# First quarters of A11 and A21 loaded apart, and the first k step's matmuls in another order

## The chip, the cores and the metric

The kernel runs on one core of a Trainium2 chip. The metric is the device time of one execution in microseconds. Three timed runs of the kernel before gave 414.72, 414.88 and 414.88 us, a median of 414.88.

The engines go by short names: TensorE is PE (its weight loads are PEld), VectorE is DVE, ScalarE is ACT, GpSimd is POOL, and SyncE, which here only issues DMAs, is SP. ACT and POOL issue DMAs too.

## The reference

The input `x` is 64 blocks of 64 x 1024 float32. Every block has a condition that picks one of 16 matrices of 64 x 64. The result is `x` plus a small feed-forward layer of the conditioned blocks:

```
W = weights[condition]                       # 64 blocks of 64 x 64
v = einsum('bct,bcd->bdt', x, W)             # conditioned input, flattened to 4096 x 1024
top1 = argmax(v @ gate_w.T + expert_bias)    # one of 4 experts for a row
z = einsum('nh,erh->ner', v, lora_A)         # 4 experts, rank 8
delta = einsum('ner,ehr->neh', z, lora_B)    # only the chosen expert's counts
out = x + v @ W_up.T + delta
```

All of it is float32.

## The kernel before

Two blocks of 64 rows make one tile of 128 rows, so there are 32 tiles (`NP`), handled as 16 pairs (`NG`). The condition is applied after the large product: for every tile the kernel first makes `x` times the joined matrix of gate, LoRA A and `W_up` (1024 x 1060, called B), and then multiplies the result by the tile's condition matrix.

For a pair of tiles the product is cut in two by rows (tile a, tile b), in two along the sum (512 each), and in two by columns (530 each, `NB`). That gives the blocks A11, A12 (tile a, first and second half of the sum), A21, A22 (tile b) and B11, B12, B21, B22. The first two pairs take the eight block products (`eight`, line 505); the others take seven with sums of blocks (`seven`, line 622). A block product runs over four k steps of 128 (`KH`), in `product` (line 214).

Float32 is done as three products: every operand is split into a high part (a rounded copy, `h...`, `ah`) and a low part (the rest, `l...`, `al`). ACT makes the high parts by a copy, DVE the low parts by a subtraction (`split_a`, `split_b`). `part_of_product` (line 198) issues the terms: term 0 is A high by B high, term 1 is A high by B low, term 2 is A low by B high. The 530 columns are done in two pieces of 264 and 266 (`BANKS`)[...]. So one k step of one block product is six matmuls, and the first k step of the first pair, which does A11 by B11 and A21 by B11 together, is twelve.

How a line is named: all engines are wrapped in `InOrder` (line 35), which keeps each engine's instructions in program order, so nearly every instruction of the trace is put down to line 43. Tile names tell them apart: `xx` holds the raw quarters of A11 and A21 (and later A12 and A22), `wraw` a raw k step of B, `hB` and `lB` the parts of B11, `ah` and `al` those of A, `c` the accumulators.

The start of the program is written out by hand. `keep_warm(WARM)` (lines 386 to 390) issues 30 matmuls of zeros on TensorE before any data is there. `load_halves` (line 393) loads, for one half of the sum and some k steps (`STEPS`, line 403), the quarters of A11 and A21 in one DMA; ACT issues the first and the second k step (lines 404 and 405), SP issues steps three and four later. SP loads B11's first k step in two pieces (lines 417 to 419), then B11's second k step, the rest of A11 and A21, the other k steps of B11, the second halves of A, and B21.

Then come the casts of the first k step, lines 436 to 450: ACT copies the first piece of B11, DVE makes A11's high part (by a maximum with itself, so that it need not wait for ACT), ACT copies the second piece of B11, DVE makes A11's low part and both low pieces of B11, ACT makes A21's high part and DVE its low part. The second k step's A follows.

The first block product is started in `run` (line 491). In `product`, with two block products at once, a k step goes: for A11 terms 0 and 2 in both pieces, then term 1 in both; then the same for A21. After the first k step the hooks of place (0, 0) in `eight` run: one more warming matmul, the split of B11's second k step, and `make_idx`, one small matmul on `condf` (the conditions, loaded by POOL into `cond_sb` at line 414 and cast by POOL), from which the row indices of the condition matrices are made.

Of the kernel before, what the change touches and what calls it, by code (L numbers as in the profile page):

```python
# [8 lines left out]
F32 = mybir.dt.float32  # L9
# [6 lines left out]
P = 128  # L16
KC = 8
KH = KC // 2
# [8 lines left out]

COLS = ((0, 356), (356, 352), (708, 352))
LAST = ((0, 356), (356, NB - 356), (NB, 258), (NB + 258, NB - 258))
WARM = 30  # L30
GATE = (("lg", E), ("mx", 1), ("sc", E), ("m2", 1), ("zm", ER))
HALVES = (slice(0, 64), slice(64, 128))

# [13 lines left out]
def kernel(  # L47
# [28 lines left out]
    tensor, vector, scalar, pool, sync = (  # L76
        InOrder(tc, e) for e in (nc.tensor, nc.vector, nc.scalar, nc.gpsimd, nc.sync)
    )
# [6 lines left out]
    yp = ctx.enter_context(tc.tile_pool(name="y", bufs=3))  # L85
# [5 lines left out]
    wh = {b: cpool.tile([P, KH, NB], F32R, name=f"h{b}") for b in BLOCKS}  # L91
    wl = {b: cpool.tile([P, KH, NB], F32R, name=f"l{b}") for b in BLOCKS}
# [3 lines left out]
    raw, As, us, ys, wsel, zs, os_, ts = ({} for _ in range(8))  # L96

    def temp(name):
        return tp.tile([P, NB], F32, name=name, tag="t")
# [23 lines left out]
    def source(g, name):  # L123
        return {
            "A11": (2 * g, 0),
            "A12": (2 * g, 1),
            "A21": (2 * g + 1, 0),
            "A22": (2 * g + 1, 1),
        }.get(name, (g, name))

    def split_a(g, name, k=slice(0, KH)):
        if (g, name) not in As:
            As[g, name] = [ap.tile([P, KH, P], F32R, name=m, tag=m) for m in ("ah", "al")]
        h, lo = As[g, name]
        src = raw[source(g, name)]
        scalar.copy(h[:, k], src[:, k])
        vector.tensor_sub(lo[:, k], src[:, k], h[:, k].bitcast(F32))


    def part(q, k):  # L140
        i, j = int(q[1]) - 1, int(q[2]) - 1
        return w[j][KH * i + k]

    def load_b(q, k):
        t = raw[q, k] = temp("wraw")
        sync.dma_start(t, part(q, k))
# [51 lines left out]
    def part_of_product(g, a, b, first, k, o, n, terms=(0, 1, 2)):  # L198
        h, lo = As[g, a]
        of = (h, wh[b]), (h, wl[b]), (lo, wh[b])  # L200
        for m in terms:
            tensor.matmul(
                o,
                of[m][0][:, k],
                of[m][1][:, k, n],
                start=first and k == 0 and m == 0,
                stop=k == KH - 1 and m == 2,
                skip_group_check=True,
            )

    BANKS = slice(0, CUT), slice(CUT, NB)
    LAST_BANKS = [slice(c0 - NB, c0 - NB + n) for c0, n in LAST[2:]]

    def product(g, which, hooks):

        turns = ((0, 1, 2),) if len(which) == 1 else ((0, 2), (1,))
        for k in range(KH):
            for c, a, b, first in which:
                for terms in turns:
                    for n in BANKS:  # L220
                        part_of_product(g, a, b, first, k, body(c)[:, n], n, terms)
            for kk, fn, *args in hooks:
                if kk == k:
                    fn(*args)

    def product_by_bank(g, places, a, b, hooks):

        for m, (o, n) in enumerate(zip(places, LAST_BANKS)):
            for k in range(KH):
                part_of_product(g, a, b, True, k, o[:, : n.stop - n.start], n)  # L230
                for kk, fn, *args in hooks:
                    if kk == KH * m + k:
                        fn(*args)

    def body(c):
        return c[:, LEFT : LEFT + NB]
# [149 lines left out]
    def keep_warm(n):  # L386
        for _ in range(n):
            tensor.matmul(wps[:, :P], warm, warm, start=True, stop=True)

    keep_warm(WARM)  # L390


    def load_halves(queue, hf, k):
        if k.start == 0:
            t = yp.tile([P, 2, KH, P], F32, name="xx", tag="y")
            for i in range(2):
                raw[i, hf] = t[:, i]
            raw["x", hf] = t
        queue.dma_start(
            raw["x", hf][:, :, k], xt[0:2, hf].rearrange("i p k q -> p i k q")[:, :, k]  # L400
        )

    STEPS = slice(0, 1), slice(1, 2), slice(2, KH)
    for k in STEPS[:2]:
        load_halves(scalar, 0, k)

    one = cpool.tile([P, 1], F32, name="one")
    vector.memset(one, 0.0)
# [2 lines left out]
    which = cpool.tile([2, P], I32, name="which")  # L411
# [7 lines left out]
    t = raw["B11", 0] = temp("wraw")  # L419
    pieces = slice(0, CUT), slice(CUT, NB)  # L420
    for n in pieces:
        sync.dma_start(t[:, n], part("B11", 0)[:, n])
    load_b("B11", 1)
    load_halves(sync, 0, STEPS[2])
    for k in range(2, KH):
        load_b("B11", k)
    load_halves(sync, 1, slice(0, KH))
    for k in range(KH):
        load_b("B21", k)
    def low(name, k):  # L430
        h, lo = As[0, name]
        vector.tensor_sub(lo[:, k], raw[source(0, name)][:, k], h[:, k].bitcast(F32))
# [3 lines left out]
    for name in ("A11", "A21"):  # L436
        As[0, name] = [ap.tile([P, KH, P], F32R, name=m, tag=m) for m in ("ah", "al")]
    t = raw["B11", 0]
    scalar.copy(wh["B11"][:, 0, p], t[:, p])
    u = raw[0, 0][:, k]  # L440
    vector.tensor_tensor(As[0, "A11"][0][:, k], u, u, ALU.max)
    scalar.copy(wh["B11"][:, 0, q], t[:, q])
    low("A11", k)
    for n in pieces:
        vector.tensor_sub(wl["B11"][:, 0, n], t[:, n], wh["B11"][:, 0, n].bitcast(F32))
    scalar.copy(As[0, "A21"][0][:, k], raw[1, 0][:, k])
    low("A21", k)
    for name in ("A11", "A21"):
        split_a(0, name, STEPS[1])

# [40 lines left out]
    def run(g, order, hooks, c):  # L491
        for s, step in enumerate(order):
            step = step if isinstance(step, list) else [step]
            for n, _, _, first in step:
                if first:
                    c[n] = chain()
            for kk, fn, *args in hooks[s]:
                if kk < 0:
                    fn(*args)
            product(g, [(c[n], l, r, first) for n, l, r, first in step], hooks[s])  # L500

    c = {}
# [328 lines left out]
```

## Time and profile before

| what | value |
|---|---|
| median of the timed runs | 414.88 us |
| profiled execution | 415.4 us |
| its span | 413.6 us |
| TensorE matmuls, busy | 408.5 us, 99% of the span |
| VectorE, ScalarE, GpSimd busy | 285.6, 185.0, 75.0 us |
| first matmul of zeros | 0.99 us |
| first matmul on data | 4.20 us |
| small matmul on `condf` | 7.26 us |
| first matmul of the second k step | 7.37 us |

The profile is of one execution, and its times count from the start of the span. A page lists the busy time of each engine, the span in slices, the chain of work that ended last, and the costliest groups of instructions. A timeline row gives the start, the duration, the engine, the line, the operation, what is written from what, the shape and the count; in brackets stands how long the engine was idle before it, and what ended the idle time. A name with a q behind the engine (SPq, ACTq) is a DMA being issued. The ends of matmuls are modelled, so durations of neighbouring matmuls overlap; the distance from start to start is what one costs.

### The profile page before, as it was taken

Reading aid. Unit: us, or ns where it says so; the run is one execution under the profiler, and the core shown is the slowest. Engines: PE = TensorE matmul, PEld = TensorE weight load, DVE = VectorE, ACT = ScalarE, POOL = GpSimd, SP = SyncE. Lnnn points to the kernel's source line nnn. Section 1 sums busy time; section 2 is a strip of 40 time slices with the busy share of each in tenths; the row PEclk is TensorE's granted clock in tenths of the full one; section 3 lists DMA queues with packets and bytes.
Section 4 is the critical chain, followed back from the end, with each engine's and each line's share of the span. In section 5 each row is a group of like instructions: output and inputs, shape, how many; then the busy total and the mean of one; then the engine's idle time right before and its main releaser. Section 6 shows DMA issues by size and latency. Waiting matters only on the chain.

```text
span 413.6 us, 8160 instructions
## 1 busy us (share of the span) xinstructions
PE 408.5 (99%) x3191; PEld 407.7 (99%) x3191; DVE 285.6 (69%) x648; ACT 185.0 (45%) x419; POOL 75.0 (18%) x92
## 2 busy tenths in 40 slices
PE   8999999999999999999999999999999999999996
PEld 8999999999999999999999999999999999999995
DVE  5987776876767666676676767666676676766766
ACT  5846734453534445333343534445333344533531
POOL 4304502020020202102020020202102020020000
PEclk9999999999999999999999999999999999999999
DMA  8889964553556435465453555434465443564345
GB/s 276 301 305 224 241 167 98 137 123 99 172 133 177 92 93 143 124 178 135 103 127 98 164 135 159 128 81 138 122 179 135 104 126 94 169 165 124 52 101 178
DMA packets 25830, 60.99 MB, mean 147 GB/s; under 512 B 3328, under 2 KB 5344, under 8 KB 25792
## 3 DMA queue, kind: packets, MB, share of 16 engines
q1 hardware_dynamic: 18112, 40.48, 27.2%
q0 software_dynamic: 6704, 19.21, 27.1%
q10 hardware_dynamic: 976, 0.79, 0.6%
q8 instruction: 25, 0.41, 0.4%
q14 instruction: 13, 0.11, 0.1%
HBM read 43.68 MB, written 16.78 MB: 146 GB/s over the span
## 4 chain that ended last, share of the span: by engine, by line
PE 97%; DMA 1%; issue 0%; POOL 0%; DVE 0%; POOLq 0%
PE c L43 81%; PE o L43 16%; DMA cond_sb<-in_cond_dram 1%; DVE y L43 0%; POOL which L43 0%; POOL condf L43 0%; POOLq L43 0%; POOLq L818 0%
## 5 line engine op out<-in xcount | busy, mean ns | idle before, releaser
L43 PE MATMUL c<-hT,ah 128*128 128x264 f32 x480 | 139.7, 291 | 0.0
L43 PE MATMUL c<-lT,ah 128*128 128x264 f32 x480 | 137.3, 286 | 0.0
L43 PE MATMUL c<-hT,al 128*128 128x264 f32 x480 | 137.1, 286 | 0.0
L43 PE MATMUL c<-hB,ah 128*128 128x264 f32 (+1 forms) x424 | 121.8, 289 | 0.0
L43 PE MATMUL c<-hB,al 128*128 128x264 f32 (+1 forms) x424 | 121.0, 287 | 0.0
L43 PE MATMUL c<-lB,ah 128*128 128x264 f32 (+1 forms) x424 | 119.0, 287 | 0.0
L43 PEld LDWEIGHTS c<-lT,ah 128*128 128x128 f32 x480 | 91.0, 190 | 0.0
L43 PEld LDWEIGHTS c<-hT,ah 128*128 128x128 f32 x480 | 90.9, 189 | 0.0
L43 PEld LDWEIGHTS c<-hT,al 128*128 128x128 f32 x480 | 90.6, 189 | 0.0
L43 POOL DMA_DIRECT2D y<-in_x_dram x31 | 29.3, 945 | 290.3 <-ACT y L43 285.3
L43 PEld LDWEIGHTS c<-hB,ah 128*128 128x128 f32 x424 | 80.7, 190 | 0.3 <-ACT hB L43 0.2
L43 PEld LDWEIGHTS c<-hB,al 128*128 128x128 f32 x424 | 80.7, 190 | 0.0
L43 PEld LDWEIGHTS c<-lB,ah 128*128 128x128 f32 x424 | 79.5, 190 | 0.2 <-issue 0.2
L43 ACT COPY y<-o 128x352 f32<-128x352 f32 (+1 forms) x91 | 40.1, 443 | 58.4 <-PE o L43 55.0
L43 ACT CAST uh<-usum 128x530 fp32r<-128x530 f32 (+4 forms) x44 | 27.1, 616 | 68.4 <-DVE usum L43 68.4
L43 DVE TENSOR_TENSOR al<-S,ah 128x512 fp32r<-128x512 f32 x56 | 38.5, 688 | 24.2 <-ACT ah L43 24.2
L43 DVE TENSOR_TENSOR al<-xh,ah 128x512 fp32r<-128x512 f32 x46 | 31.7, 689 | 30.0 <-ACT ah L43 30.0
L43 PE MATMUL o<-uh,bd 128*128 128x356 f32 (+2 forms) x186 | 44.7, 322 | 0.0
L43 DVE TENSOR_TENSOR ul<-usum,uh 128x530 fp32r<-128x530 f32 (+4 forms) x44 | 30.0, 682 | 18.6 <-ACT uh L43 18.6
L43 ACT CAST zt<-o 96x128 fp32r<-96x128 f32 x31 | 8.1, 262 | 76.0 <-PE o L43 76.0
L43 POOL DMA_INDIRECT wsel<-in_cw_dram,idx x32 | 34.9, 1089 | 10.6 <-issue 5.2
L43 ACT CAST ah<-S 128x512 fp32r<-128x512 f32 x56 | 34.9, 623 | 1.8 <-DVE S L43 1.4
(88 smaller groups left out, 471.3 us busy)
## 6 DMA issues: line engine op xcount, KB each, us to landing
xh<-in_xt_dram SPq DMA_DIRECT2D x60, 256.0 KB
y<-in_x_dram POOLq DMA_DIRECT2D x30, 512.0 KB, 5.6
out_dram<-y SPq DMA_DIRECT2D x30, 512.0 KB
wraw<-in_w_dram SPq DMA_DIRECT2D x23, 265.0 KB
T<-in_w_dram POOLq DMA_DIRECT2D x8, 265.0 KB, 7.3
xx<-in_xt_dram SPq DMA_DIRECT2D x1, 512.0 KB
wsel<-in_cw_dram,idx POOLq DMA_INDIRECT x32, 5.0
y<-in_x_dram SPq DMA_DIRECT2D x1, 512.0 KB
```

The costliest lines, as they stand in the source:

```text
L43: return lambda *a, **k: self.tc.keep_in_program_order(fn(*a, **k))
```

## The change

The first quarters of A11 and A21 are loaded by two DMAs instead of one, both still issued by ACT. The second quarters, still one DMA for both, are issued by SP, between the second piece of B11's first k step and B11's second k step. `WARM` goes from 30 to 26. The casts of the first k step are put in another order on ACT and DVE: A21's high part comes before the second piece of B11 on ACT, A21's low part before the second low piece of B11 on DVE. The twelve matmuls of the first k step are issued by a new function, `first_step`, in a written order; each entry is the block product (0 is A11, 1 is A21), the piece and the terms. Their number and operands are the same.

```diff
-WARM = 30
+WARM = 26
...
         for k in range(KH):
-            for c, a, b, first in which:
-                for terms in turns:
-                    for n in BANKS:
-                        part_of_product(g, a, b, first, k, body(c)[:, n], n, terms)
+            if g == 0 and k == 0 and which[0][2] == "B11":
+                first_step(which)
+            else:
+                for c, a, b, first in which:
+                    for terms in turns:
+                        for n in BANKS:
+                            part_of_product(g, a, b, first, k, body(c)[:, n], n, terms)
...
+    def first_step(which):
+
+        p, q = BANKS
+        for m, n, terms in (
+            (0, p, (0, 2)),
+            (1, p, (0,)),
+            (0, p, (1,)),
+            (1, p, (1,)),
+            (0, q, (0, 2)),
+            (1, q, (0,)),
+            (1, p, (2,)),
+            (1, q, (2,)),
+            (0, q, (1,)),
+            (1, q, (1,)),
+        ):
+            c, a, b, _ = which[m]
+            part_of_product(0, a, b, True, 0, body(c)[:, n], n, terms)
...
-    for k in STEPS[:2]:
-        load_halves(scalar, 0, k)
+
+    def load_first(i):
+        if i == 0:
+            raw["x", 0] = yp.tile([P, 2, KH, P], F32, name="xx", tag="y")
+        t = raw[i, 0] = raw["x", 0][:, i]
+        scalar.dma_start(t[:, STEPS[0]], xt[i, 0][:, STEPS[0]])
+
+    for i in range(2):
+        load_first(i)
...
         sync.dma_start(t[:, n], part("B11", 0)[:, n])
+    load_halves(sync, 0, STEPS[1])
     load_b("B11", 1)
...
-    scalar.copy(wh["B11"][:, 0, p], t[:, p])
+
+    def low_b(n):
+        vector.tensor_sub(wl["B11"][:, 0, n], t[:, n], wh["B11"][:, 0, n].bitcast(F32))
+
     u = raw[0, 0][:, k]
     vector.tensor_tensor(As[0, "A11"][0][:, k], u, u, ALU.max)
+    scalar.copy(wh["B11"][:, 0, p], t[:, p])
+    low("A11", k)
+    scalar.copy(As[0, "A21"][0][:, k], raw[1, 0][:, k])
+    low_b(p)
     scalar.copy(wh["B11"][:, 0, q], t[:, q])
-    low("A11", k)
-    for n in pieces:
-        vector.tensor_sub(wl["B11"][:, 0, n], t[:, n], wh["B11"][:, 0, n].bitcast(F32))
-    scalar.copy(As[0, "A21"][0][:, k], raw[1, 0][:, k])
     low("A21", k)
+    low_b(q)
```

More of the change, by code (lines that the diff above doesn't have):

```diff
@@ L393, in load_halves @@
     def load_halves(queue, hf, k):
-        if k.start == 0:
+        if ("x", hf) not in raw:
             t = yp.tile([P, 2, KH, P], F32, name="xx", tag="y")
```

## The prediction

> **What bounds the kernel now.** I read the page from the top: engines, then the chain that ended last.
>
> ```profile
> PE 408.5 (99%) x3191; PEld 407.7 (99%) x3191; DVE 285.6 (69%) x648; ACT 185.0 (45%) x419; POOL 75.0 (18%) x92
> ...
> PE 97%; DMA 1%; issue 0%; POOL 0%; DVE 0%; POOLq 0%
> PE c L43 81%; PE o L43 16%; DMA cond_sb<-in_cond_dram 1%; DVE y L43 0%; POOL which L43 0%; POOL condf L43 0%; POOLq L43 0%; POOLq L818 0%
> ```
>
> TensorE is busy for 99% of the span and is 97% of the chain. Its matmuls follow each other 0.12 us apart, and from 9.95 us on I find no step between two matmuls that is a wait on data of more than 0.1 us. So after 10 us the change can move nothing: the number of real matmuls is the same. It can move only the moment at which the gapless stream begins. The chain restricted to the first 9 us tells what sets that moment:
>
> ```profile
> 1.40 5.55 DMA cond_sb<-in_cond_dram
> 6.95 0.05 issue
> 7.01 0.21 POOL condf L43
> 7.22 0.04 issue
> 7.26 0.17 PE o L43
> 7.43 1.60 PE c L43 x11
> ```
>
> Until 7.26 us the chain is not the quarters of A or B11, but the little load of the conditions (`cond_sb`, line 414), whose cast `condf` feeds the one matmul of `make_idx`. That matmul stands in TensorE's order right behind the first k step. The timeline of the same stretch shows the first step in front of it:
>
> ```profile
> 3.39 0.41 ACT L43 CAST hB<-wraw 128x264 fp32r<-128x264 f32 x1 [0.15 <-DMA wraw<-in_w_dram]
> 3.76 0.38 SPq L43 DMA_DIRECT2D xx<-in_xt_dram  x1
> 3.76 0.29 DVE L43 TENSOR_TENSOR ah<-xx 128x128 fp32r<-128x128 f32 x1 [2.13 <-DMA xx<-in_xt_dram]
> ...
> 4.20 0.56 PE L43 MATMUL c<-hB,ah 128*128 128x264 f32 x1
> ...
> 6.76 0.73 ACT L43 CAST hB<-wraw 128x264 fp32r<-128x264 f32 x2 [1.57 <-DMA wraw<-in_w_dram]
> 6.88 0.10 PEld L43 LDWEIGHTS <-warm 128*128 128x128 bf16 x1
> 6.88 0.23 PE L43 MATMUL o<-warm 128*128 128x128 bf16 x1
> ...
> 7.26 0.17 PE L43 MATMUL o<-condf,batch 2*128 2x32 bf16 x1
> ...
> 7.36 0.19 PEld L43 LDWEIGHTS c<-hB,ah 128*128 128x128 f32 x1 [0.23 <-ACT hB L43]
> ```
>
> The first step's twelve matmuls start at 4.20 and are through at 6.88. Then TensorE stands until 7.26 for `condf`, and at 7.36 for the second k step's B11, which landed at 6.73. Both are late for one reason: of a DMA's sixteen completion counts, fifteen had come by 5.16 (`cond_sb`) and 5.33 (B11, k=1), and the last one, of a single one of the 16 DMA engines, came at 6.95 and 6.73. The third quarter's B11 is alike: fifteen by 6.86, the last at 8.13; its low part (8.83 + 0.71) then holds a matmul at 9.60. Small holds of 0.10, 0.06, 0.12 and 0.11 us lie between 7.36 and 9.95, 0.39 in all.
>
> **The change, part by part.**
>
> Loads. The 16 DMA engines took p (132 KB), the pair of first quarters (128 KB), q and the pair of second quarters in this order; they landed at 3.36, 3.74, 4.15 and 4.54, about 0.39 us apart, so the traffic is bound by bytes. A11's first quarter is now 64 KB alone: it should land half a pair's time earlier, 3.74 - 0.19 = 3.55. Bounds: 3.36 (with p) and 3.74 (no gain). A21's quarter follows at 3.74 or, if q is served first, 4.15; the second quarters are next and all bytes before B11, k=1 are the same as before, so it comes at 6.73 again, and `cond_sb`, which POOL issues untouched at 1.40, at 6.95.
>
> Issue time. ACT issues two DMAs of 128x128 for two of 128x2x128 (0.47 and 0.49 us; the nearest rows, SP's pieces of B11, are 0.38 and 0.42), so its table load starts some 0.15 earlier; ACT then idles for p anyhow (the 0.15 above). SP has one issue more, 0.42 to 0.49: B11, k=1 goes out at 2.12 instead of 1.65, the third and fourth quarters of A at 2.6 for 2.12, B11 k=2 and 3 at 3.1 and 3.6. B11, k=3 now waits for the completion eight DMAs back, A11's quarter (3.55, so no wait in fact); the next load, which waited until 3.75, and those behind it slip by 0.3 to 0.4. All this is hidden by the backlog: the first packets of B11, k=1 moved at 3.69 and those of A's third and fourth quarters at 4.49, two microseconds after their issue. Were the backlog gone, it would cost up to 0.47 on B11, k=1.
>
> DVE and ACT. A11's high part (0.29) runs 3.57 to 3.86, its low part ends at 4.19 (the same 0.33 step as at 3.76 and 4.09), the low part of p follows to 4.53. ACT does A21's high part after p, so q's cast must wait for A21: 4.12 if A21 came first, about 4.34 if q did, against 4.17 before. Behind that wait on ACT stand q's cast and the casts of the second quarters, and for q wait its low part on DVE and the sixth product on TensorE. Cost 0 to 0.17 on q; the sixth product comes at 5.20, q's cast ends by 4.75, so it is covered.
>
> TensorE. WARM falls by 4 matmuls, 0.107 us each: warming ends at 3.74 instead of 4.17. First product at 3.86 + 0.08 = 3.94 (4.20 before). In the new order: A11's low part 4.30, A21 high 4.54, low p 4.76 and 4.98, then no operand is late any more: seven more at 0.22 each, the twelfth at 6.52 instead of 6.75. Full speed begins at about 6.65 (below), so the step is through at 6.68, 0.20 us earlier than 6.88. The bounds of this gain are 0 (A11 at 3.74) and 0.30 (A11 with p).
>
> The sum on the path: the step is earlier by 0.20, TensorE then stands 0.20 longer for `condf`, 7.26 stays, 9.60 stays. 415.4 (profiled: span 413.6 and 1.8 around it) + 0 = 415.4; the timed median is 0.5 below the profiled execution, which gives 414.9.
>
> The clock is where a loss could come from, and the one place where a page speaks against the change. The granted-clock column of the windows reads 1.00 from the start, but the steps between equal matmuls are 0.220 us up to 6.58 and 0.12 after; the record of full clock starts at 6.65. The Trainium skill, "TensorE: Matmul & The Clock Gate", "Part 1: The HAM clock gate", says the array runs at half rate until a free-running window of about 3.4 us has been busy. Here a window that ended at 3.24 would have been busy for 2.25 of 3.41 us (66%) and did not open the clock; 3.24 to 6.65 had about 0.2 us of holes (94%) and did. With WARM at 26 the holes are 0.2 between warming and first product, and 0.15 to 0.2 more behind it: 88 to 89%. No row has a price between 66 and 94%. By the rows (nearest to 94%) the term is 0; by the strict reading of the rule's "sustained" it is a window more of half rate. I take 0 and keep the other end as a rival.
>
> **Rivals.**
>
> A, hidden (the forecast): 414.9, own range 414.7 to 415.1.
>
> B, the cover is absent in timed runs. The timed runs are 0.5 us shorter than the profiled one, and without the late sixteenth engine the stream would begin 0.28 + 0.39 = 0.67 earlier. If that is where the 0.5 went, nothing hides the first step, and its 0.20 is seen: 414.7, at most 414.6. Against it: nothing in the trace says that the late engine belongs to profiling.
>
> C, slower: the holes keep the clock at half for another window, to 6.65 + 3.41 = 10.06. From 7.36 matmuls then take 0.22 instead of 0.12: 2.7 us at half rate lose 1.35, less up to 0.39 of holds which disappear in it: 1.0 to 1.35, so 415.9 to 416.2 (an estimate; the window's length is the page's). It decides once the busy share needed lies above 88%.
>
> D, the lateness goes away because the order of descriptors is another: 0.67 + 0.20 off, 414.0. No cause for the lateness is visible in the trace, so neither is its cure.
>
> E, the late engine gets later: one packet of B11, k=1 took 1.22 us where 0.087 is usual; another such costs up to 1 us: 415.9.
>
> **How the numbers follow.** A 0.52, B 0.28, C 0.12, D 0.05, E 0.03. The time is A's. The range 414.4 to 415.4 holds A, B and the mild cases of C and E, and leaves out D and the full C. 0.2% is 0.83 us, about what a measurement of this kernel can tell from no change. Only most of D is faster by that (0.04); C and E mostly pass it on the slow side (0.11); the rest, 0.85, is within.
>
> **What would show it.** DVE's wait for the first quarter should end near 3.55 for 3.76, the first product stand at 3.94, the step end near 6.7, and `condf`'s matmul still stand near 7.26 with a longer idle before it: then A is right. If the second k step starts at 7.0 or earlier, the cover is not fixed (B or D). If steps of 0.22 us go on after 7.4, it is C. If A11 lands at 3.74 all the same, the term of the loads is wrong, though not the time. The prediction as a whole fails if `condf` or B11, k=1 move by more than 0.8 us, or the clock opens a window later.

## The result: slightly slower, and the profile after

| | before | after |
|---|---|---|
| median of the timed runs | 414.72 us (22 runs, 414.5 to 415.6) | 415.57 us (22 runs, 415.14 to 416.14) |
| ratio | | 1.0017, 95% interval 1.0011 to 1.0023 |
| profiled execution (its span) | 415.4 us (413.6) | 415.85 us (414.1) |

The kernel became slower by 0.85 us in the medians, 0.17 us beyond the upper end of the range; the ratio makes the loss 0.7 us. It is small, but its interval excludes no change.

The page of the kernel after: engines, and the shares of the chain that ended last.

```profile
PE 408.3 (99%) x3187; PEld 406.6 (98%) x3187; DVE 285.8 (69%) x648; ACT 185.3 (45%) x419; POOL 74.9 (18%) x92
...
PE 97%; DMA 1%; SPq 0%; DVE 0%; ACT 0%; issue 0%
PE c L43 81%; PE o L43 16%; DMA wraw<-in_w_dram 1%; SPq L43 0%; DVE y L43 0%; ACT hB L43 0%
```

TensorE has four matmuls fewer (the warming ones) and is as busy as before. What changed is the name in third place: the chain no longer begins with the conditions (`cond_sb`), it begins with loads of B and with SP's issuing. The same chain, restricted to the first 10 us (start, duration, what):

```profile
1.66 0.43 SPq L43
2.08 0.04 issue
2.12 4.33 DMA wraw<-in_w_dram
6.46 0.02 issue
6.48 0.42 ACT hB L43
6.90 0.04 issue
6.95 3.16 PE c L43 x21
```

The issue at 1.66 is the new one, the second quarters. Behind it B11's second k step (B11, k=1) goes out at 2.12 instead of 1.65, and its landing at 6.46 starts the stream of matmuls at 6.95. The timeline of the kernel after shows both sides, the early part that went as it was meant to and the wait behind it:

```profile
1.66 0.43 SPq L43 DMA_DIRECT2D xx<-in_xt_dram  x1
...
2.12 0.47 SPq L43 DMA_DIRECT2D wraw<-in_w_dram  x1
...
3.62 0.29 DVE L43 TENSOR_TENSOR ah<-xx 128x128 fp32r<-128x128 f32 x1 [1.98 <-DMA xx<-in_xt_dram]
...
4.06 0.56 PE L43 MATMUL c<-hB,ah 128*128 128x264 f32 x1
...
4.11 0.43 SPq L43 DMA_DIRECT2D xx<-in_xt_dram  x1
...
6.09 0.18 PE L43 MATMUL o<-condf,batch 2*128 2x32 bf16 x1
...
6.95 0.39 PE L43 MATMUL c<-hB,ah 128*128 128x264 f32 x1 [0.67 <-ACT hB L43]
```

The first product is 0.14 us earlier than before (4.06 for 4.20), the first k step ends earlier, and the small matmul on `condf` stands at 6.09, not at 7.26. Up to here this execution is ahead: matching the two streams of matmuls one by one, the second k step's first matmul is 0.42 us earlier than before, and the one that stood at 9.60 is 0.37 us earlier. Then the lead is lost and more. TensorE's weight loads of the kernel after, around 12 us, with their waits in brackets:

```profile
11.95 0.19 PEld L43 LDWEIGHTS c<-hB,ah 128*128 128x128 f32 x1 [0.21 <-ACT hB L43]
...
12.69 0.30 PEld L43 LDWEIGHTS c<-lB,ah 128*128 128x128 f32 x2 [0.20 <-DVE lB L43]
...
13.29 0.19 PEld L43 LDWEIGHTS c<-hB,al 128*128 128x128 f32 x1 [0.18 <-DVE al L43]
```

Before had no wait in this stretch. The second halves of A (A12 and A22, one DMA) are issued at 4.11 instead of 3.76 and their cast on ACT starts at 10.59 instead of 10.20. The low parts that DVE makes of these halves, and the parts of B behind them in DVE's order, come later by as much. A12's cast, A22's low part and the weight load that reads this low part, first before, then after:

```profile
10.20 0.62 ACT L43 CAST ah<-xx 128x512 fp32r<-128x512 f32 x1 [0.55 <-issue]
...
12.19 0.69 DVE L43 TENSOR_TENSOR al<-xx,ah 128x512 fp32r<-128x512 f32 x1
...
12.93 0.19 PEld L43 LDWEIGHTS c<-hB,al 128*128 128x128 f32 x1
```

```profile
10.59 0.62 ACT L43 CAST ah<-xx 128x512 fp32r<-128x512 f32 x1 [0.73 <-DMA xx<-in_xt_dram]
...
12.56 0.69 DVE L43 TENSOR_TENSOR al<-xx,ah 128x512 fp32r<-128x512 f32 x1
...
13.29 0.19 PEld L43 LDWEIGHTS c<-hB,al 128*128 128x128 f32 x1 [0.18 <-DVE al L43]
```

The difference between the streams goes from -0.37 at 9.6 to +0.36 at 13.5 and stays +0.36 to the last matmul.

The transfers themselves look different too. The windows view gives busy time by engine for a stretch; its last three columns are granted clock, DMA share and GB/s. First before, then after:

```profile
3.00:4.00 1.00, 1.00 (x12) 1.00 (x11) 0.24 (x1) 0.64 (x3) 1.00 (x5) 1.00 1.19 361
4.00:5.00 1.00, 1.00 (x7) 0.94 (x5) 0.97 (x5) 0.82 (x4) 0.23 (x5) 1.00 0.99 311
5.00:6.00 1.00, 1.00 (x7) 1.00 (x6) 0.67 (x4) 0.19 (x1) 0.00 (x0) 1.00 1.08 368
```

The same view of the kernel after:

```profile
3.00:4.00 1.00, 0.95 (x9) 0.68 (x7) 0.34 (x2) 0.56 (x2) 1.00 (x5) 1.00 1.07 265
4.00:5.00 1.00, 0.94 (x5) 0.97 (x6) 0.98 (x4) 0.62 (x2) 0.23 (x5) 1.00 0.78 101
5.00:6.00 1.00, 1.00 (x10) 0.95 (x9) 0.34 (x2) 0.39 (x2) 0.20 (x1) 1.00 0.93 331
```

Between 4 and 5 us the traffic falls from 311 to 101 GB/s, although B11, k=1 had been issued at 2.12 and the two DMAs behind it by 3.2. By 5.0 us, 609 KB have arrived instead of 843. The DMA share of 0.78 in that row says that the engines were not idle: their packets took long. (A packet is what one DMA engine moves at once, here mostly one row of a load.) A packet of B11's second k step, 2120 bytes, usually takes 0.087 us. Of the packets that started between 2.5 and 7 us in the kernel after, 20, all of this size, took over 0.3 us more than packets of their size usually do, 12.6 us more together, or 0.8 us for each of the 16 engines. Before had five such slow packets (2.9 us together).

### The profile page after: what moved, and what is told of

The parts are those of the page before. It is cut to its first block, busy times and chain, and to the rows that moved or that the text cites. A ratio compares the mean times of both kernels' runs of the same rounds, so it can differ in the third digit from the quotient of the medians.

```text
span 414.1 us, 8155 instructions
## 1 busy us (share of the span) xinstructions
PE 408.3 (99%) x3187; PEld 406.6 (98%) x3187; DVE 285.8 (69%) x648; ACT 185.3 (45%) x419; POOL 74.9 (18%) x92
## 4 chain that ended last, share of the span: by engine, by line
PE 97%; DMA 1%; SPq 0%; DVE 0%; ACT 0%; issue 0%
PE c L43 81%; PE o L43 16%; DMA wraw<-in_w_dram 1%; SPq L43 0%; DVE y L43 0%; ACT hB L43 0%
```

## The experiments

Three theories were tried one after the other; the expectations name them. The **queue** theory: the second quarters were better off on ACT's queue, and SP is one DMA too full. The **cover** theory: ACT's DMAs of 256 KB in all had kept the DMA engines busy while SP's wait to flow; with only 128 KB on ACT nothing covers that time. The **place** theory: what counts is the place in SP's order; a DMA more ahead of B11, k=1, whatever it carries, sends that load and all behind it out 0.47 us later. Their rivals are the new order of casts and matmuls, the shorter warming, and single causes named below. Ratios are against the kernel before, measured on the same chip, with the 95% interval. "KB by 5.0" counts what had arrived 5 us into the profiled execution, to within some 5 KB; each kernel has one profile.

### Which edit costs it

**Second quarters on ACT's queue again**, behind the two first quarters (the rest as in the kernel after).

```diff
     for i in range(2):
         load_first(i)
+    load_halves(scalar, 0, STEPS[1])
...
-    load_halves(sync, 0, STEPS[1])
     load_b("B11", 1)
```

> The changed kernel with its second quarters issued by ACT again, behind the two first quarters; SP has the issues of the kernel before. Queue theory (the second quarters on SP's queue put B11's second k step alone in line, and its first packets stall): the traffic runs on through 4 to 5 us, A12 lands near 10.2 and the time is 414.5 to 414.8, though ACT's third issue puts its table load some 0.45 us later. Split theory (two small DMAs in place of a pair cost the time): 415.5. Order theory (casts, matmul order, WARM): 415.5.

Measured 416.21 us (before 414.87), 1.0044 [1.0028, 1.0059]: the largest ratio of the study. Of its seven runs three took 417.4 to 417.7, with a mean granted clock of 0.994 where the others have 0.999 or more; the other four took 415.5 to 416.2, still slower than before. What set the three apart was not found. The dip in the traffic is gone (841 KB by 5.0), but half of the second quarters' completion counts had come by 5.16 and the last at 6.70, and behind them on ACT stood the casts of B11, k=1. The timeline of that kernel:

```profile
6.73 0.50 ACT L43 CAST ah<-xx 128x128 fp32r<-128x128 f32 x2 [2.19 <-DMA xx<-in_xt_dram]
7.13 0.72 ACT L43 CAST hB<-wraw 128x264 fp32r<-128x264 f32 x2
```

So the queue theory missed: its cure brings another wait.

**Only the second quarters on SP**, all else as before.

```diff
-    for k in STEPS[:2]:
-        load_halves(scalar, 0, k)
+    load_halves(scalar, 0, STEPS[0])
...
         sync.dma_start(t[:, n], part("B11", 0)[:, n])
+    load_halves(sync, 0, STEPS[1])
     load_b("B11", 1)
```

> The kernel before with one thing changed: the pair of second quarters is issued by SP behind the pieces of B11's first k step. Queue theory: the dip of the traffic at 4 to 5 us is there, 415.3 to 415.7. Split theory: 414.7. Order theory: 414.7.

Measured 415.62 us (414.87), 1.0017 [1.0009, 1.0024]; 617 KB by 5.0. This one edit gives the whole loss.

**Only the orders**: the loads of the kernel before, the casts, matmul order and `WARM` of the kernel after.

```diff
-    def load_first(i):
...
+    for k in STEPS[:2]:
+        load_halves(scalar, 0, k)
...
-    load_halves(sync, 0, STEPS[1])
     load_b("B11", 1)
```

> The loads of the kernel before, with the changed kernel's casts, matmul order and WARM of 26. Queue theory and split theory: 414.7, as before. Order theory, by the clock or by the casts: 415.4 or more, with steps of 0.22 us between matmuls beyond 7.4 us if it is the clock.

Measured 415.21 us (414.87), 1.0009 [1.0001, 1.0018]. It profits nothing, and seems to lose 0.3 us; the cause of that was not found. Its profile has no dip (948 KB by 5.0), and its stream is 0.67 us ahead of before's at 8.9 us, but only 0.16 us ahead from 13.2 us on, after waits for A12 and A22 (landed at 10.03). In this execution the earlier start is thus lost again at the next load.

**The old warming** in the kernel after.

```diff
-WARM = 26
+WARM = 30
```

> The changed kernel with WARM at 30 again. Queue theory and split theory: 415.5, no gain, and the dip of the traffic once more. If the shorter warming is the cause: 414.7.

Measured 415.57 us (414.87), 1.0015 [1.0007, 1.0022]; 667 KB by 5.0. The shorter warming is not the cause.

### What about that edit: place, cover, queue or first touch

**Second quarters on SP, but behind B11, k=1.**

```diff
-    for k in STEPS[:2]:
-        load_halves(scalar, 0, k)
+    load_halves(scalar, 0, STEPS[0])
...
     load_b("B11", 1)
+    load_halves(sync, 0, STEPS[1])
     load_halves(sync, 0, STEPS[2])
```

> The kernel before with the second quarters issued by SP, but behind B11's second k step and not ahead of it. Cover theory (B11's second step has no second hardware queue beside it while its first packets stall): the dip of the traffic at 3.5 to 5 us is there again, 115 to 250 GB/s in the worst half microseconds, A12 lands at 10.5 and the time is 415.3 to 415.7. Small-rows theory (it is the 512-byte rows of the second quarters in SP's own queue that choke what comes next): B11's second step lands undisturbed near 5.3, a dip comes later if at all, and the time is 414.7 to 415.0.

Measured 415.46 us (414.71), 1.0016 [1.0009, 1.0022]; 731 KB by 5.0. B11, k=1 is back at 1.65, lands at 5.82, and nothing is gained: now the second quarters are late (6.30), and the loads behind both go out at the later times all the same. So the additional issue need not stand ahead of B11, k=1 to cost its time.

**A twin on ACT**: second quarters on SP as above, and ACT loads the same 128 KB once more into a buffer that nobody reads.

```diff
+    load_halves(scalar, 0, STEPS[0])
+    twin = xp.tile([P, KH, P], F32, name="xh", tag="xh")
+    scalar.dma_start(
+        twin[:, :2], xt[0:2, 0].rearrange("i p k q -> p i k q")[:, :, 1]
+    )
...
+    load_halves(sync, 0, STEPS[1])
     load_b("B11", 1)
```

> The second quarters on SP's queue ahead of B11's second step, and beside them a load of the same 128 KB by ACT's queue into a buffer that nobody reads. It adds 128 KB, some 0.35 us of traffic. Cover theory: with packets in a second queue the traffic runs on at over 300 GB/s through 4 to 5 us; A12 lands near 10.2 + 0.35 less or equal to the dip that is saved, and the time is 414.9 to 415.3. Small-rows theory: the dip stays and the extra bytes come on top, 415.8 to 416.1.

Measured 415.10 us (414.71), 1.0011 [1.0003, 1.0019]; 812 KB by 5.0, of which 128 are the twin's. The stretch from 4 to 5 us carries 282 GB/s. The dip is filled and the loss somewhat smaller, but the point estimates' difference to the kernel without the twin (1.0017) lies within the intervals. This spoke for the cover theory, until the run with a small issue below.

**The conditions by ACT instead of POOL**, second quarters on SP.

```diff
+    cond_sb = cpool.tile([2, NP], I32, name="cond_sb")
+    scalar.dma_start(cond_sb, cond)
...
-    cond_sb = cpool.tile([2, NP], I32, name="cond_sb")
-    pool.dma_start(cond_sb, cond)
...
+    load_halves(sync, 0, STEPS[1])
     load_b("B11", 1)
```

> The second quarters on SP's queue ahead of B11's second step, and the load of the conditions issued by ACT in place of POOL, so that no software queue is at work in the first 8 us. Cover theory: the dip is there all the same, 415.4 to 415.7 (a load of 256 bytes gives no cover). Software-queue theory (POOL's descriptors stall the engines at 3.9 to 5.2): no dip, 414.6 to 414.9.

Measured 415.36 us (414.71), 1.0016 [1.001, 1.0023]; 621 KB by 5.0: the dip stays, so POOL's DMA between the others is not its cause.

**A touch**: second quarters on SP, and ACT reads the first 64 bytes of every row of B11, k=1 beforehand, into a buffer that nobody reads.

```diff
+    twin = xp.tile([P, KH, P], F32, name="xh", tag="xh")
+    scalar.dma_start(twin[:, 0, :16], part("B11", 1)[:, :16])
...
+    load_halves(sync, 0, STEPS[1])
     load_b("B11", 1)
```

> The second quarters on SP's queue ahead of B11's second k step, and by ACT's queue a read of the first 64 bytes of each of the 128 rows of that k step (8 KB, into a buffer that nobody reads), so that its memory has been read once before its load comes. First-touch theory (the dip is the slow first reading of a new region): the dip goes, 414.7 to 415.0. Cover theory without first touch (it takes a second queue with traffic): the dip stays, 415.3 to 415.7.

Measured 415.55 us (414.90), 1.0019 [1.0013, 1.0026]; 602 KB by 5.0. That these rows are read for the first time is not the cause either.

**Second quarters by ACT behind its table load.** In fact the DMA went out at 1.72, while the table load ran.

```diff
     scalar.copy(one, one)
+    load_halves(scalar, 0, STEPS[1])
...
-    load_halves(sync, 0, STEPS[1])
     load_b("B11", 1)
```

> The changed kernel with the second quarters issued by ACT, behind its table load and its first copy (from about 3.1 us), instead of by SP. Cover theory: these 128 KB flow in the second queue from 4 us on, beside B11's second k step, so the traffic does not dip below 250 GB/s: 414.5 to 414.8, with the cast of p up to 0.15 late behind the issue. If a second queue is of no use at that time, 415.4 or more.

Measured 415.94 us (414.90), 1.0026 [1.0015, 1.0037]. As in the first experiment the second quarters' last count came late (6.71) and held ACT's casts.

### Is it the second halves of A?

**A12 and A22 in two DMAs**, with B21's first k step between them; the kernel before otherwise.

```diff
-    load_halves(sync, 1, slice(0, KH))
-    for k in range(KH):
+    t = yp.tile([P, 2, KH, P], F32, name="xx", tag="y")
+    for i in range(2):
+        raw[i, 1] = t[:, i]
+        sync.dma_start(t[:, i], xt[i, 1])
+        if i == 0:
+            load_b("B21", 0)
+    for k in range(1, KH):
         load_b("B21", k)
```

> The kernel before with the pair of A12 and A22 loaded in two, A12 first, then B21's first k step, then A22. If the landing of this pair (10.2 in the kernel before, 10.56 in the changed one) is what sets the stream beyond 12 us, then A12's cast starts 0.6 to 0.7 earlier and the second bound goes away; what is left is the landing of B11's k steps: 414.3 to 414.7. If the pair is covered in the kernel before, no change: 414.8 to 414.9.

Measured 414.58 us (414.71), 1.0000 [0.9991, 1.0008]: no change. (The execution that was profiled took 413.94, the least of its 13 runs.)

**The same edit in the kernel after.**

```diff
-    load_halves(sync, 1, slice(0, KH))
...
+        sync.dma_start(t[:, i], xt[i, 1])
+        if i == 0:
+            load_b("B21", 0)
...
```

> The changed kernel with the pair of A12 and A22 loaded in two, with B21's first k step between. In its profile the stream started 0.37 us ahead of the kernel before and then lost 0.73 us between 11.9 and 13.5, waiting for what this pair feeds. If that loss is the path of the changed kernel in general, it goes: 414.9 to 415.2. If the late landing of B11's k steps holds the stream as long, it stays at 415.4 to 415.7.

Measured 415.40 us (414.90), 1.0017 [1.001, 1.0023]. A12's cast now starts at 9.35 instead of 10.59. The ratio is that of the kernel after, and in the medians 0.50 us of its 0.85 remain. So the waits around 12 us, on which the profile after puts the loss, are only the last of a row: with them gone the stream of this profile is held by B11, k=1 (landed at 6.59), 0.21 us ahead of before's at 13.5 us. The profiled execution showed where one execution lost its time, not what all of them lose.

That row can be followed in the profiles of other kernels. In four of them it is the pair A12 and A22 that holds the stream, and the stream from 13.5 us on is as late as A12's cast:

| kernel | A12's cast starts | weight load held by A22's low part | stream from 13.5 us, against before |
|---|---|---|---|
| after | 10.59 | 13.29 | +0.36 |
| touch | 10.18 | 12.91 | -0.03 |
| B11's second k step in two (below) | 10.03 | 12.73 | -0.20 |
| only the orders | 10.06 | 12.78 | -0.16 |

From the cast to the weight load it is 2.70 to 2.73 us in all four, and 2.73 in before (10.20 and 12.93): before was at this limit without a wait that would have shown it.

**Both**: second quarters by ACT behind the table load, and A12 and A22 apart.

```diff
     scalar.copy(one, one)
+    load_halves(scalar, 0, STEPS[1])
...
-    load_halves(sync, 0, STEPS[1])
...
-    load_halves(sync, 1, slice(0, KH))
...
+        sync.dma_start(t[:, i], xt[i, 1])
+        if i == 0:
+            load_b("B21", 0)
...
```

> The second quarters by ACT behind its table load, and A12 and A22 loaded apart, on the changed kernel. If the cover and the pair are the two things that hold the stream, both are gone: 413.8 to 414.4, better than both kernels. If the cover theory is wrong: 415.0 to 415.5.

Measured 416.12 us (414.90), 1.0036 [1.0024, 1.0048]: nothing gained here either.

### One issue more, one issue fewer

**B11's first k step in one DMA** in the kernel after, so that B11, k=1 is SP's third DMA again (1.65).

```diff
-    for n in pieces:
-        sync.dma_start(t[:, n], part("B11", 0)[:, n])
+    sync.dma_start(t, part("B11", 0))
     load_halves(sync, 0, STEPS[1])
```

> The changed kernel with B11's first k step in one DMA, so that B11's second step is SP's third DMA again, as in the kernel before, while ACT's queue still carries only 128 KB. Place theory (an early DMA moves some 2.6 us after its issue whatever lies ahead, and an issue takes 0.47 us; what counts is how many KB stand in SP's first three and ACT's first two): 128 + 265 + 128 + 265 = 786 KB, as in the kernel before, so 780 KB or more are through by 5.0 us and there is no dip; 414.6 to 415.0. Cover theory (it takes a second queue with traffic): ACT's queue is dry by 3.6, the dip is there, some 600 KB by 5.0, 415.4 to 415.7.

Measured 416.61 us (414.89), 1.0035 [1.0025, 1.0045]. Its runs fall into two groups, three of 415.00 to 415.37 and eleven of 416.24 to 417.14; the profiled one (416.27) is of the second. The traffic is healed: 859 KB by 5.0 with 128 KB on ACT only, B11, k=1 landed at 5.20. The time is not, for a reason of its own. The timeline of that kernel:

```profile
3.93 0.41 ACT L43 CAST hB<-wraw 128x264 fp32r<-128x264 f32 x1 [0.78 <-DMA wraw<-in_w_dram]
...
4.58 0.56 PE L43 MATMUL c<-hB,ah 128*128 128x264 f32 x1 [0.63 <-DVE ah L43]
...
8.24 0.42 PE L43 MATMUL c<-hB,al 128*128 128x264 f32 x1
...
8.46 0.42 PE L43 MATMUL c<-hB,ah 128*128 128x266 f32 x1
```

B's first cast waits for the whole k step, the first product stands at 4.58, a hole of 0.8 us behind the last warming matmul, and matmuls still start 0.22 us apart at 8.46. Full speed began at 8.8.

**The same with a warming of 34**, which closes the hole.

```diff
-WARM = 26
+WARM = 34
...
-    for n in pieces:
-        sync.dma_start(t[:, n], part("B11", 0)[:, n])
+    sync.dma_start(t, part("B11", 0))
```

> The run with p and q in one DMA on the changed kernel, with WARM at 34 so that the warming reaches its later first product at 4.57 (26 left a hole of 0.8 us, and its clock opened at 8.8 us). Place theory: SP issues B11's second step as its third DMA again, so the loss is gone but for the later first product: 414.7 to 415.1. If the second quarters on SP cost the time by themselves, 415.5; if the clock is not what spoiled that run, 416.3 or more.

Measured 415.33 us (414.95), 1.0011 [1.0005, 1.0018], with full speed from 5.63 and 925 KB by 5.0. The hole had cost 1.3 us (416.61 - 415.33); what is left of the loss is 0.4 us, about half of that of the kernel after, at a first product that is still later (4.62) than before's. That is 0.2 us more than the place theory had allowed.

**B11, k=1 in two DMAs**, the kernel before otherwise: one issue more on SP, no byte moved.

```diff
-    load_b("B11", 1)
+    t1 = raw["B11", 1] = temp("wraw")
+    for n in pieces:
+        sync.dma_start(t1[:, n], part("B11", 1)[:, n])
     load_halves(sync, 0, STEPS[2])
```

> The kernel before with B11's second k step loaded in two pieces of 132 and 133 KB, so that SP has one issue more ahead of what follows; ACT's queue carries both pairs, 256 KB, as before. Place theory: 653 KB stand in the first places, 650 to 740 KB are through by 5.0, everything behind slips by 0.45, 415.1 to 415.6. Cover theory: ACT's queue is as before, 840 KB by 5.0, 414.7 to 414.9.

Measured 415.52 us (414.89), 1.0018 [1.0011, 1.0024]. The time is what the place theory said. Its profile shows no dip (874 KB by 5.0, 291 GB/s from 4 to 5 us); that execution took 415.11, the least of its runs.

**One small issue**: the kernel before, and SP loads 8 KB into a buffer that nobody reads, ahead of B11, k=1. Both pairs of quarters stay with ACT.

```diff
         sync.dma_start(t[:, n], part("B11", 0)[:, n])
+    twin = xp.tile([P, KH, P], F32, name="xh", tag="xh")
+    sync.dma_start(twin[:, 0, :16], part("B11", 1)[:, :16])
     load_b("B11", 1)
```

> The kernel before with one more DMA issued by SP, 8 KB into a buffer that nobody reads, between B11's first and second k steps; ACT's queue and everything else as before. Place theory (an issue more ahead of B11's second step costs the time, whatever it carries): 415.3 to 415.7. Cover theory (ACT's second pair makes good for it) and any theory that counts bytes: 414.8 to 415.0.

Measured 415.54 us (414.95), 1.0015 [1.0009, 1.0022]; 615 KB by 5.0. Its windows and, in a fence of their own, SP's rows in the timeline:

```profile
3.00:4.00 1.00, 1.00 (x12) 1.00 (x11) 0.36 (x2) 0.63 (x3) 1.00 (x5) 1.00 1.48 295
4.00:5.00 1.00, 1.00 (x8) 1.00 (x7) 1.00 (x4) 0.98 (x4) 0.45 (x6) 1.00 0.65 92
5.00:6.00 1.00, 1.00 (x6) 1.00 (x6) 0.53 (x3) 0.03 (x1) 0.00 (x0) 1.00 0.78 288
```

```profile
1.65 0.42 SPq L43 DMA_DIRECT2D xh<-in_w_dram  x1
...
2.12 0.44 SPq L43 DMA_DIRECT2D wraw<-in_w_dram  x1
...
2.60 0.43 SPq L43 DMA_DIRECT2D xx<-in_xt_dram  x1
```

This refutes the cover theory: ACT's 256 KB are there, eight kilobytes were added, and the loss in the median (0.59 us) and the dip are near those of the kernel after. One issue of 0.42 us at this place suffices. The execution that was profiled took 416.27, the most of its 21 runs, so its dip may be deeper than usual; the loss does not rest on it. As in the kernel after, 20 slow packets make the dip (14.7 us together).

**One issue fewer**: the kernel before with B11's first k step in one DMA.

```diff
-    for n in pieces:
-        sync.dma_start(t[:, n], part("B11", 0)[:, n])
+    sync.dma_start(t, part("B11", 0))
     load_b("B11", 1)
```

> The kernel before with B11's first k step in one DMA. Place theory: all that SP issues behind it moves 0.47 earlier, the third and fourth quarters start near 4.2 instead of 4.7 and A12 and A22 land up to 0.45 earlier; the first product waits for the whole of B11's first step, at most 0.4, and is covered by the later wait for B11's second step: 414.2 to 414.6. Cover theory: nothing gained, 414.7 to 415.1.

Measured 415.08 us (414.89), 1.0004 [0.9997, 1.001]. Less issuing buys nothing: here, and in the next run, the place theory's forecast failed.

**The same with A12 and A22 apart.**

```diff
-    for n in pieces:
-        sync.dma_start(t[:, n], part("B11", 0)[:, n])
+    sync.dma_start(t, part("B11", 0))
...
-    load_halves(sync, 1, slice(0, KH))
...
+        sync.dma_start(t[:, i], xt[i, 1])
+        if i == 0:
+            load_b("B21", 0)
...
```

> As the run before it, and A12 and A22 loaded apart with B21's first k step between. Place theory: both bounds of the stream move, 413.8 to 414.4. Cover theory: 414.6 to 415.0.

Measured 414.79 us (414.89), 0.9998 [0.999, 1.0006]. No kernel of the study is measurably faster than the one before.

### The landings together

When the last of the 16 completion counts of a load came, in us, in the profiled execution of each kernel (without the three in which the second quarters, issued by ACT, held ACT's casts). Slow packets are counted as above, from 2.5 to 7 us.

| kernel | B11, k=1 issued | B11, k=1 landed | B11, k=2 landed | slow packets | loss in the median |
|---|---|---|---|---|---|
| before | 1.65 | 6.73 (15 counts by 5.33) | 8.13 (15 by 6.86) | 5 | |
| only the orders | 1.65 | 5.35 | 6.62 | 0 | 0.34 |
| A12 and A22 apart | 1.65 | 5.21 | 6.90 | 5 | -0.13 |
| after | 2.12 | 6.46 | 7.77 | 20 | 0.85 |
| only second quarters on SP | 2.12 | 7.08 | 8.48 | 8 | 0.75 |
| warming of 30 | 2.12 | 7.22 | 8.55 | 15 | 0.70 |
| conditions by ACT | 2.12 | 6.82 | 8.15 | 10 | 0.65 |
| touch | 2.12 | 6.39 | 7.74 | 13 | 0.65 |
| after, A12 and A22 apart | 2.12 | 6.59 | 7.94 | 19 | 0.50 |
| twin on ACT | 2.12 | 6.36 | 8.04 | 4 | 0.39 |
| second quarters behind B11, k=1 | 1.65 | 5.82 | 7.68 | 12 | 0.75 |
| B11, k=1 in two | 1.65 and 2.12 | 4.88 and 5.76 | 7.11 | 6 | 0.63 |
| one small issue | 2.12 | 6.41 | 8.87 | 20 | 0.59 |
| after, B11's first k step in one | 1.65 | 5.20 | 7.91 | 14 | 1.72 |
| the same, warming of 34 | 1.65 | 5.44 | 7.31 | 6 | 0.38 |
| one issue fewer | 1.18 | 4.80 | 7.12 | 6 | 0.19 |
| one fewer, A12 and A22 apart | 1.18 | 4.82 | 6.94 | 2 | -0.10 |

The first three rows issue these loads alike. Two of the three have no late count: 5.35 and 5.21. Against those two, the rows with B11, k=1 (or its second part) at 2.12 have B11, k=1 between 0.4 and 2.0 us later and B11, k=2 between 0.2 and 2.3, mostly more than the 0.47 us that the issue takes. An issue fewer brings k=1 forward by 0.4 to 0.55 us, and k=2 not at all (7.12 and 6.94 against 6.62 and 6.90). Where the packets start shows the same. With the third and fourth quarters of A issued at 1.65 or 2.12 a tenth of their packets had started by 4.55 to 4.73 (both kernels with an issue fewer, only the orders, A12 and A22 apart, before); issued at 2.6 they started at 5.02 to 5.50 in eight kernels, at 4.80 with the second quarters behind B11, k=1, and only with B11, k=1 in two no later than before, at 4.62. So earlier than in before, something else than SP's issuing sets the start and the landing; later, the loads behind mostly come later. How much of that is the later issue itself is not shown: nearly all the profiles with late starts have more slow packets in front of these loads (8 to 20; the twin's has 4, but 128 KB more to move) than before and the kernels with its issues or fewer (0 to 6; 14 in the kernel after with B11's first k step in one DMA). Where the issue is late and slow packets are few, as with B11, k=1 in two (6), the start is not late. That what sets the start at the earlier issues is the number of bytes (the stretch from 4 to 5 us carries 377 GB/s in the kernel with only the orders) is likely, and was not tested.

## Why the prediction was wrong

**What held.** A11's first quarter landed at 3.59 (forecast 3.55), the first product stood at 4.06 (3.94). The step was through at 5.92 (6.68); that it was so early is luck, since full speed began at 4.66 in this execution, not at 6.65. Four warming matmuls fewer did no harm. The order of casts and matmuls gained nothing, as forecast.

**The step that failed** is the one on issue time: "All this is hidden by the backlog: the first packets of B11, k=1 moved at 3.69 and those of A's third and fourth quarters at 4.49, two microseconds after their issue." The two microseconds were read as a queue of bytes that swallows half a microsecond of later issue at no cost. In the kernel after it did not: the third and fourth quarters, issued at 2.63 instead of 2.12, started at 5.24 instead of 4.73, 2.61 us after their issue both times, and the traffic in front of them ran at 101 GB/s from 4 to 5 us. The same step had the right term in its next sentences, "Were the backlog gone, it would cost up to 0.47 on B11, k=1", and put it at nothing. Measured, the term is 0.6 to 0.75 us in the six kernels that take the loads of before and give SP one early issue more (two of them also change or add a small DMA on ACT; with the 128 KB twin it was 0.39). Part of it is probably not the issue's own time but the slow packets that come with it in nearly all these profiles; that split was not tested.

**What the term was hidden behind on paper.** "7.26 stays, 9.60 stays" took the late sixteenth counts of one execution for a property of the kernel. Of the three kernels with these early loads only the profile of before has them, and the small matmul moved to 6.09 after. Rival B's premise (the cover is absent in timed runs) was therefore probably the better reading (no profile shows it for the timed runs themselves), and its conclusion was wrong: without the cover it is not the first step's gain of 0.20 that shows, it is the lateness of the loads behind. The hint was in the numbers: the timed median lay 0.5 us below the profiled execution.

**"From 9.95 us on I find no step between two matmuls that is a wait on data", so "after 10 us the change can move nothing"** was wrong as well. No wait is not the same as slack. In before, A22's low part was made by DVE from 12.19 to 12.88 for a weight load at 12.93, 0.05 us later; after, it was made from 12.56 to 13.25 and the weight load, which waited for it, came 0.04 us later. So there was next to no slack. The prediction had found that these loads "slip by 0.3 to 0.4" and did not follow that to who reads them: the issue slipped by 0.35, the cast by 0.39, and between the two profiled executions the stream by 0.36.

**The other rivals.** C (the clock) did not happen in the kernel after: its full speed began at 4.66. But it exists: with B11's first k step in one DMA, whose warming ends 0.8 us before the first product, full speed began at 8.8, and closing the hole brought 1.3 us back, close to C's 1.0 to 1.35. The runs also narrow the busy share that C turns on, worked out with the window of 3.41 us that the prediction takes (both shares are estimates from the starts of the matmuls). With the second quarters behind B11, k=1 full speed began at 3.67; matmuls had run from 0.99 on, 79% of the window that ended there, and this was enough. With the hole, the window that ended at 5.39, one ahead of the opening at 8.8, was busy for about 70%, and this was not. So the 88% of the prediction lay on the safe side. D did not come about as a gain: B11, k=1 landed at 6.46, with its fifteenth count as late as 6.41. E is nearer to what the trace shows than its chance of 0.03: it took one packet of 1.22 us for a sign that more could come, and in the profile of the kernel after there are 20 slow packets, not on one engine's account but 0.8 us for each of the 16. Whether they come as often in the timed runs is not known.

**What stays open.** By which route the issue costs its time, and whether the slow packets are what takes the loss (0.5 to 0.85 us) beyond the 0.47 us of the issue; why an issue more makes packets slow from 4 to 5 us (the software queue, the first touch and the missing cover are excluded as the only cause); and why the kernel with B11, k=1 in two loses as much with no such dip in its profile; and the 0.3 us of the kernel with only the orders. With one profile for each kernel, and late counts that differ from execution to execution, the landings above show the direction, not the size.

## What to carry to other kernels

Near the start of a program the issuing engine can be a serial resource on the path: count the DMAs ahead of the first loads that TensorE will wait for, and charge an additional one its full issue time, even if the data seem to queue for two microseconds behind it. The reverse does not follow: one issue fewer gained nothing here. A wait that hides something in one profiled execution is cover only if other executions have it; where the timed median lies below the profiled time, work out the sum without that wait. And where the stream shows no waits, look at how early each operand is made before calling a later load free.

## What was not expected of the hardware

- One DMA more in SP's order (0.42 to 0.47 us to issue) cost 0.6 to 0.75 us, whether it carried 128 KB, 8 KB, or half of a load that was there anyway. The Trainium skill, "DMA: Bandwidth & Descriptors", "Issuing engines are not separate DMA queues", says that issuing from several engines saves only the sequencer's time to initiate a DMA, "which is usually small relative to the DMA itself". Here that time was what decided, and moving the DMA to ACT's queue was no way out: the last count then came at 6.70, in front of ACT's casts.
- With an issue more, packets of B11, k=1 became slow: 0.087 us is usual, and in the profiles of the kernel after and of the small issue 18 each took from 0.4 to 1.4 us. The DMA share of 0.78 and 0.65 at 101 and 92 GB/s shows the same: a low rate of bytes was not idle time.
- The time from issue until a tenth of the packets had started was 2.0 to 3.0 us for the third and fourth quarters of A, and 3.1 to 3.9 us for the second halves, in kernels with and without the dip.
- The clock of TensorE opened between 3.67 and 6.65 us in the profiled executions whose warming had no large hole, and their times do not follow it (6.65 us and 415.4 before, 4.66 and 415.85 after). The Trainium skill, "TensorE: Matmul & The Clock Gate", "Part 1: The HAM clock gate", has a free-running window as the reason and puts the spread at 0.5 us to either side; here it was 3 us. The granted-clock column shows 1.00 all the while; the steps between equal matmuls (0.22 and 0.12 us) tell.
- A single one of the 16 completion counts can come 1.3 to 1.8 us after the fifteenth (before: `cond_sb` 5.16 and 6.95; B11, k=2 6.86 and 8.13), where the kernel with only the orders, with the same loads, has at most 0.1 us for both.
